# The opening of a sixteen-batch attention kernel: TensorE in text order from its first instruction, and the first batch laid out anew

## The chip, the cores and the metric

The kernel runs on one core of one Trainium2 chip. A core has five engines that run side by side, each through its own instructions in a fixed order, and wait for each other through semaphores: TensorE (PE: matrix products and transposes, weight loads shown apart as PEld), VectorE (DVE), ScalarE (ACT), GpSimd (POOL) and SyncE (SP). Transfers are started by SP, and where rows are picked by an index by GpSimd. The metric is the time of one execution on the device in microseconds (us); less is better. Three runs of the kernel before took 963.57 to 964.73 us, with a median of 963.98.

## The reference

For each of 16 batches with 1024 tokens of width 512, it computes masked self-attention with 8 heads of 64, in which one projection serves as query, key and value, and adds the result to the input:

```python
xt = jnp.transpose(x, (0, 2, 1))
q = xt @ Wq.T
qh = q.reshape(B, T, NH, dk).transpose(0, 2, 1, 3)
scores = scale * jnp.einsum('bhqd,bhkd->bhqk', qh, qh)
cmask = mask[:, None, None, :]
rmask = mask[:, None, :, None]
logits = (scores * cmask + (1.0 - cmask) * NEG) * rmask
attn = jax.nn.softmax(logits, axis=-1)
ctx = jnp.einsum('bhqk,bhkd->bhqd', attn, qh)
ctx = ctx.transpose(0, 2, 1, 3).reshape(B, T, D)
out = ctx @ Wo.T
return jnp.transpose(out, (0, 2, 1))
```

`x` is (16, 512, 1024), the mask (16, 1024) holds zeros and ones, about half of each, and the two weights are 512 x 512. A token whose mask is 0 is no key for anybody; as a query it sees all tokens alike, so its row is the mean.

## The kernel before

**What it does with the mask.** Only tokens with mask 1 ("active") need attention. For each batch the kernel puts the active tokens in front, gathers their rows of `x` from HBM by index (four gathers of 128 rows, and a fifth for a tail where more than 512 are kept), computes attention for 512, 528 or 544 slots and scatters the finished rows back. Rows of masked tokens get the mean instead. Batches run in order of their number of active tokens, so that the widths `wide` can be fixed: the first and the last two are 512 wide.

**The opening** (`run`, up to the loop over batches). The mask arrives; `order` counts the active tokens with eight products of a matrix of ones, forms a key (count times 32 plus the batch's number) and, comparing all keys with all, the rank of each batch. `permute` picks the mask of the batch with a given rank, by a one-hot of the rank; `sources` the number of that batch. `slots_of` turns a mask into slots, by products with a triangular matrix and with ones; `hot` compares each token's slot within its block of 128 with 0 to 127 (one operation on 128 x 1024), and `index` multiplies these one-hots with the token numbers, which gives the list of rows, `idx`. Then come the gathers of batch 0, the transposes `xt` (into two buffers of the pool `ps_0`, then split in a high and a low half of 16 bits, `xh` and `xl`, by `xsplit`), and the query products `query(b, e, g)`: head pair `e`, half `g` of the tokens, 12 products of 16-bit halves each. `qsplit` splits a head pair of q again and spreads it over `xx` by four transfers. `value` transposes q back for the values and sums their squares per head; `peaks`, `top`, `bottom` (together `shift`) take the largest square per head, transpose it, take the largest, and spread it with its sign changed as `nm`: the exponent's bias. `warm` issues products of ones without use, 30 of them, which keep TensorE busy while it has to wait. Meanwhile ScalarE and VectorE split the weights (`wqh`, `wql`), and `sum_half` sums x over the tokens for the mean.

**The loop.** For a batch, `scores(b, p, u)` computes head pair `p` against half of the keys, four tiles that lie over four and a bit of six accumulator banks (`pss`), and four exponentials on ScalarE, each with a running sum; `attend` multiplies these with the values, into banks 4 and 5; `tail_scores` and `attend_tail` do the slots over 512. `recip_sums` and `recip_rows` make one over the sums and bring them to all partitions through HBM (`rr`, `rd`, `rb`), `norm` applies them, `project` multiplies with the output weights and scatters. While batch b runs, the transposes, query products and values of b+1 and the lists of b+2 are put between its scores, by `plan`: 18 steps, each with two places, `(step, half)`. `free` holds what is started at the beginning of a step.

**What sets the order.** A scheduler of the language orders the instructions of an engine by priority and by estimated times; `behind` and `high_priority` steer it, and `once` or `needs` add a wait. From the first score on, TensorE is taken out of it (`manual_schedule`): its instructions stand as the text issues them. In the opening it is the scheduler's. Small products in the loop use a spot in bank 5 (`spot`) or one of two buffers of `ps_m` (`pm`), which they share with the big products.

Waits between `scores` and the exponentials on the same banks: the first product of `scores` waits for the four exponentials before (`self.left`), and the exponentials wait for all products of their `scores`.

## Time and profile before

| | |
|---|---|
| median of three runs | 963.98 us (963.57 to 964.73) |
| profiled execution | 965.21 us, span 963.5 us |
| instructions | 22790 |
| TensorE busy | 931.5 us (97%), 8121 products |
| VectorE busy | 721.1 us (75%) |
| ScalarE busy | 644.7 us (67%) |
| GpSimd busy | 305.1 us (32%) |
| transfers | 176.30 MB, mean 183 GB/s |

The profile is of one execution on the chip. The span runs from the first to the last instruction. A row of the timeline gives the start, the length, the engine, the line of the source and the tile written and read, `tile<-tiles`; in brackets stands how long the engine was idle before and what ended it. A row of waits gives who waited for whom, the sum, how many times, and the longest. A row of stretches gives the busy time of each engine between two moments. Lengths of products overlap, since they are pipelined: twelve that take 0.27 us each start 0.11 us apart.

### The profile page before, as it was taken

What the parts mean: (1) busy time and instruction counts of PE and PEld (TensorE: products, weight loads), DVE (VectorE), ACT (ScalarE), POOL (GpSimd) and SP (SyncE); (2) the same over time, 40 slices, a digit from 0 to 9 for tenths busy, and PEclk for the clock granted to TensorE, in tenths of its full rate; (3) what the DMA queues carried; (4) which work ended last, traced back from release to release, by engine and by line L of the source; (5) the groups of instructions that cost most, each with busy time, mean ns of one, the idle gap of its engine ahead of it and who ended that gap; (6) DMA issues with size and microseconds to landing.
All of it is one profiled execution on the core that took longest, in us unless ns stands there. A gap on an engine that the chain in (4) does not pass through costs nothing.

```text
span 963.5 us, 22790 instructions
## 1 busy us (share of the span) xinstructions
PE 931.5 (97%) x8121; PEld 581.3 (60%) x8121; DVE 721.1 (75%) x2443; ACT 644.7 (67%) x1669; POOL 305.1 (32%) x311
## 2 busy tenths in 40 slices
PE   6799999999999999999999999999999999999997
PEld 4556656566666666666666566666666666565543
DVE  7779677776777767887678687877877788685563
ACT  4778766667677666776767678665767866665651
POOL 2102022142241513415144250522515135252452
PEclk9999999999999999999999999999999999999999
DMA  5756556556675666756656787654767757555552
GB/s 172 222 175 203 155 154 183 163 180 190 180 209 148 194 197 193 220 157 199 177 181 204 198 239 223 177 158 136 214 168 233 243 144 207 151 161 161 171 175 102
DMA packets 78568, 176.30 MB, mean 183 GB/s; under 512 B 14480, under 2 KB 22416, under 8 KB 78448
## 3 DMA queue, kind: packets, MB, share of 16 engines
q1 hardware_dynamic: 57392, 107.09, 39.8%
q0 software_dynamic: 21056, 67.68, 22.4%
q8 instruction: 66, 1.08, 0.5%
q14 instruction: 54, 0.44, 0.2%
HBM read 91.36 MB, written 33.91 MB: 130 GB/s over the span
## 4 chain that ended last, share of the span: by engine, by line
PE 81%; DVE 10%; ACT 4%; DMA 2%; issue 2%; SPq 1%; POOL 0%; POOLq 0%; DVEq 0%; ACTq 0%
PE pss L858 22%; PE pss L823 17%; PE pm L982 17%; PE pm L591 16%; ACT p L838 2%; PE pss L876 2%; PE pm L562 2%; DMA xx<-hl 1%; PE pss L766 1%; PE pm L654 1%; DVE xl L521 1%; PE pss L982 1%; DVE xa L988 1%; PE pm L912 1%; DVE p L777 1%
## 5 line engine op out<-in xcount | busy, mean ns | idle before, releaser
L838 ACT ACTIVATE p<-pss,nm 128x528 f32<-128x528 f32 (+2 forms) x512 | 353.9, 702 | 104.7 <-PE pss L823 101.5
L858 PE MATMUL pss<-p,v 128*64 128x264 f32 (+2 forms) x2048 | 242.4, 389 | 0.0
L823 PE MATMUL pss<-xx 128*128 128x118 f16 (+17 forms) x1856 | 213.6, 287 | 3.9 <-ACT p L838 2.8
L1051 POOL DMA_INDIRECT y_out<-xa,idx x68 | 82.0, 1206 | 405.2 <-DVE nq L732 85.1
L858 PEld LDWEIGHTS pss<-p,v 128*64 128x64 f32 x2048 | 141.4, 137 | 85.8 <-issue 4.9
L823 PEld LDWEIGHTS <-xx 128*128 128x128 f16 (+1 forms) x1856 | 103.2, 96 | 85.1 <-issue 34.3
L591 PE MATMUL pm<-xh,wqh 128*128 128x264 f16 (+5 forms) x512 | 141.8, 277 | 3.3 <-DVE xl L521 1.3
L591 PE MATMUL pm<-xh,wql 128*128 128x264 f16 (+5 forms) x512 | 141.1, 275 | 0.0
L591 PE MATMUL pm<-xl,wqh 128*128 128x264 f16 (+5 forms) x512 | 140.9, 275 | 0.0
L591 PEld LDWEIGHTS <-wqh 128*128 128x128 f16 x1024 | 96.4, 97 | 31.6 <-issue 12.6
L458 POOL DMA_INDIRECT xa<-x_in,idx x68 | 72.5, 1066 | 123.4 <-DMA y_out<-xa,idx 49.1
L838 ACT ACTIVATION_READ_ACCUMULATOR p<-pss,nm 128x1 f32 x512 | 105.2, 205 | 0.0
L982 PE MATMUL pm<-woh,ch 128*128 128x512 f16 x240 | 91.1, 380 | 0.0
L982 PE MATMUL pm<-woh,cl 128*128 128x512 f16 x240 | 90.9, 379 | 0.0
L982 PE MATMUL pm<-wol,ch 128*128 128x512 f16 x240 | 90.9, 379 | 0.0
L595 ACT ACTIVATE q<-pm 128x264 f32<-128x264 f32 (+5 forms) x128 | 50.8, 397 | 43.1 <-PE pm L591 42.7
L988 DVE SCALAR_TENSOR_TENSOR xa<-pm,xa 128x512 f32<-128x512 f32 x61 | 41.6, 681 | 46.0 <-PE pm L982 45.7
L1051 POOL DMA_INDIRECT y_out<-xi,idx x60 | 64.9, 1081 | 33.9 <-PE pss L766 13.4
L658 ACT COPY v<-pm 128x512 f32<-128x512 f32 x64 | 37.5, 586 | 56.0 <-PE pm L654 54.3
L982 PEld LDWEIGHTS <-ch 128*128 128x128 f16 x480 | 44.9, 98 | 47.5 <-issue 4.1
L458 POOL DMA_INDIRECT xi<-x_in,idx x60 | 59.4, 990 | 21.6 <-issue 15.8
L881 ACT COPY c<-pss 128x528 f32<-128x528 f32 (+2 forms) x64 | 38.3, 598 | 37.9 <-PE pss L876 26.8
(249 smaller groups left out, 1485.0 us busy)
## 6 DMA issues: line engine op xcount, KB each, us to landing
xm<-x_nat_in SPq DMA_DIRECT2D x60, 512.0 KB
xx<-hl SPq DMA_DIRECT2D x208, 136.0 KB
rb<-rd SPq DMA_DIRECT2D x72, 132.0 KB
xx<-hl SPq DMA_DIRECT2D x48, 128.0 KB
pt<-c SPq DMA_DIRECT2D x36, 132.0 KB
pt<-p SPq DMA_DIRECT2D x36, 132.0 KB
rb<-rd SPq DMA_DIRECT2D x32, 136.0 KB
ub<-ud SPq DMA_DIRECT2D x16, 256.0 KB
```

The source lines that it names most:

```text
L458: dma = self.nc.gpsimd.indirect_dma_start(out=tile[:n], out_offset=None, in_=self.x, in_offset=bass.IndirectOffsetOnAxis(ap=idx, axis=0))
L562: self.pe = nc.tensor.transpose(pt[:, c, :], x[:n, c * P:(c + 1) * P], self.ident[:n, :n]).ins
L591: self.beat = nc.tensor.matmul(pq, lhsT=w[:, c, e * P:(e + 1) * P], rhs=xx[:, c, cols], start=(k == 0), stop=(k == 3 * DC - 1)).ins
L595: nc.scalar.activation(s["q"][:, e, cols], pq, AF.Copy, scale=1.0 / (SX * SW))
L658: nc.scalar.copy(v, pv)
L823: m = nc.tensor.matmul(flat[:, c0:c1], lhsT=w, rhs=x, start=banks[n] not in banks[:n], stop=banks[n] not in banks[n + 1:])
L838: e = nc.scalar.activation(t, flat[:, at:at + A], AF.Exp, bias=s["nm"][p // 2][:, p % 2 * 2 + k:p % 2 * 2 + k + 1], scale=SCALE, accum_out ...
L858: mm = nc.tensor.matmul(pav[k * DK:(k + 1) * DK, g], lhsT=s["v"][p][:, i, k * DK:(k + 1) * DK], rhs=ps[k, i][:, cols], start=(i == 3), sto ...
L881: self.context_out = nc.scalar.copy(c[:, :A].rearrange("p (g c) -> p g c", g=2), pav).ins
L982: mm = nc.tensor.matmul(po[:cols.stop - cols.start], lhsT=a[:, e, cols], rhs=w[:, e, :], start=(e == 0 and k == 0), stop=(e == DC - 1 and ...
L988: return self.nc.vector.scalar_tensor_tensor(x, po, 1.0 / (SX * SW), x, ALU.mult, ALU.add).ins
L1051: dma = self.nc.gpsimd.indirect_dma_start(out=self.out, out_offset=bass.IndirectOffsetOnAxis(ap=idx, axis=0), in_=x, in_offset=None)
```

## The change

It touches the opening, the first batch, and a few places of all batches.

- TensorE is in text order from its first instruction (`manual_schedule` moves ahead of `order`). The text of the opening is rearranged to be that order, with 22 warm-ups instead of 30.
- Batch 0's mask comes from the least key, not from the ranks: `least` is the smallest key, `is_equal` with it picks the mask. Its number follows as the least key minus 32 times its count, in `slots_of`. The ranks (`ranks`) and `sources` of the others come later.
- In `slots_of` the one-hot comparison of 128 x 1024 becomes eight of 128 x 128 with a scalar per partition, and each of the eight products of `index` waits for its own.
- `slots_of(1)` stands behind the first transposes; the constants of `setup3` (`quad`, `two`, `par`, `low`, `sign`) get a place of their own in the text. The values of head pairs 0 and 1 of batch 0 go to `ps_0`, behind the query products of pair 1. The five gathers of batch 1 come after the query products of pair 2.
- The largest score of batch 0 (`peaks` and `top`, then `bottom`) is issued between its first score products, after the second and the sixth (`between`).
- In batch 0 (`alone`) a score product that begins a bank waits for the exponential of that bank only, exponentials for the products of their own bank only, and they are issued as the banks get done.
- `slots` and `facts_end` use the spot in bank 5 rather than a `pm` buffer, with the reads ahead of other work; `seen` notes these reads.
- The loads of `wo` and of x for the sums, in batch 0, wait for the last product issued (`beat`) rather than for the largest score, and those of `wo` go to steps 3, 6, 9, 12.
- For every batch but the last, `recip_rows` of head pair 1 moves from the head of step 10 to behind the query product in `(10, 0)` (batch 0: `(11, 0)`), as `turn`. Slots move from `(6, 0)` to `(7, 1)`, and in batch 0 a few places are shifted.

```diff
@@ order
+        self.key = key
+        nc.vector.tensor_reduce(self.least, key, AX.X, ALU.min)
+        each = self.sb([P, TB, B], F16, "hl", 2)
+        nc.vector.scalar_tensor_tensor(each, key.unsqueeze(1).broadcast_to([P, TB, B]), self.least,
+                                       mh.rearrange("p b j -> p j b"), ALU.is_equal, ALU.mult)
+        with nc.allow_low_precision(reason="one of the terms is 0 or 1, the others are 0"):
+            nc.vector.tensor_reduce(self.act16[:, 0], each, AX.X, ALU.add)
+
+    def ranks(self):
+        nc, B, key = self.nc, self.B, self.key
         more = self.sb([P, B, B], F16, "c", 4)
...
@@ slots
-        pr = self.pm([P, B, TB])
...
+        spot = self.spot(NC + B)
+        pr, pn = spot[:, :NC].rearrange("p (b j) -> p b j", j=TB), spot[:, NC:]
...
@@ slots_of
+        if b == 0:
+            who = self.base[:, 0:1]
+            nc.vector.scalar_tensor_tensor(who, n, -32.0, self.least, ALU.mult, ALU.add)
+            nc.vector.tensor_copy(self.first_row[:, 0:1], who[0:1, :])
+            nc.vector.tensor_scalar(who, who, float(T), None, ALU.mult)
...
-        nc.vector.tensor_tensor(self.oht[:, b], oh, self.tok.unsqueeze(2).broadcast_to([P, TB, NB]), ALU.mult)
+        for j in range(TB):
+            nc.vector.tensor_scalar(ol[:, j], self.io128, lo[:, j:j + 1], None, ALU.is_equal)
+            if j == 2:
+                nc.vector.tensor_tensor(self.oht[:, b], oh, self.tok.unsqueeze(2).broadcast_to([P, TB, NB]), ALU.mult)
@@ facts_end
-        pe = self.pm([P, B])
-        nc.tensor.matmul(pe, lhsT=self.on16, rhs=self.whole_masks, start=True, stop=True)
+        pe = self.spot(B)
+        self.spotted(nc.tensor.matmul(pe, lhsT=self.on16, rhs=self.whole_masks, start=True, stop=True))
...
@@ value
-        pv = self.pm([P, 4, P])
+        pv = self.pm([P, 4, P]) if b or e > 1 else self.ps_0.tile([P, 2, D], F32, tag="s", name="pss")[:, 0].rearrange("p (k n) -> p k n", k=4)
@@ scores
+            if alone and self.left:
+                own = (1, 2, 3, 0)[banks[n]]
+                if banks[n] not in banks[:n]:
+                    self.needs(m.ins, self.left[own])
+                self.other_banks(m.ins, *(e for k, e in enumerate(self.left) if k != own))
+            elif n == 0 and self.left:
                 self.needs(m.ins, *self.left)
             last = [m.ins]
+            mms.append(m.ins)
+            if n in self.between:
+                self.between.pop(n)()
...
+            if alone:
+                self.other_banks(e, *(m for m, bank in zip(mms, banks) if bank != j))
@@ attend
-                    self.other_banks(mm.ins, *exps[1 - g:])
-                    if g == 0 and i == 3:
+                    self.other_banks(mm.ins, *exps[(1 - g) * (self.reach > 512):])
+                    if g == 0 and i == 3 and self.reach > 512:
                         self.needs(mm.ins, *exps[:1])
@@ run: the opening
+        stack = ExitStack()
+        stack.enter_context(self.tc.manual_schedule(engines={mybir.EngineType.PE}))
         with self.tc.high_priority(offset=HPO):
             self.order()
-            self.permute(0, 1)
-            self.active(0, 1)
-            self.sources(0, 2)
             self.slots_of(0)
-            self.hot(0)
-        self.warm(6)
+        self.warm(7)
         self.index(0)
...
+        self.warm(12)
+        sums0 = [(0, L(self.sum_half, 0, k)) for k in range(2 * DC)]
+        for _, f in sums0[:4]:
+            f()
+        self.xt(0, 0)
+        with self.tc.high_priority(offset=HPO):
+            self.slots_of(1)
+        self.setup3()
+        self.warm(1)
+        self.xt(0, 1)
+        self.warm(2)
+        self.xt(0, 2)
...
-        first = query(0, 0, 0) + xt(0)[3:] + [(0, L(self.facts, 0, 2))] + query(0, 1, 0) + query(0, 0, 1)
-        sums0 = [(0, L(self.sum_half, 0, k)) for k in range(2 * DC)]
-        split1 = query(0, 1, 1)[1:]
-        first += [(0, index1)] + sums0[:4] + value(0, 0) + g1[:1] + query(0, 1, 1)[:1] + g1[1:2]
-        first += value(0, 1) + split1 + sums0[4:] + query(0, 2, 0) + g1[2:3] + query(0, 2, 1)[:1] + g1[3:4]
-        first += [(0, shift0)]
+        first = query(0, 0, 0) + xt(0)[3:] + query(0, 1, 0) + [(0, index1)] + query(0, 0, 1) + [(0, one_sum)]
+        first += query(0, 1, 1) + value(0, 0) + value(0, 1) + sums0[5:] + query(0, 2, 0) + query(0, 2, 1)[:1] + g1
+        first += [(0, L(self.sources, 2, B))]
...
+        self.between = {1: largest, 5: told}
@@ run: the loop
+                turn = [(0.1, L(self.recip_rows, b, 1))]
...
-                                (5, 1): vt(b, 1) + pk(b, 1), (6, 0): post,
-                                (7, 0): third + q(1, 0) + tp(b, 1), (7, 1): q(1, 1) + P_(0) + bt(b, 1), (8, 0): tc(0) + v(0) + end + rng[:2],
-                                (10, 0): tv(0) + tail + q(2, 0), (11, 0): hot + rng[2:] + early,
+                                (5, 1): vt(b, 1) + pk(b, 1),
+                                (7, 0): third + q(1, 0) + tp(b, 1), (7, 1): q(1, 1) + post + P_(0) + bt(b, 1), (8, 0): tc(0) + v(0) + end + rng[:2],
+                                (10, 0): tv(0) + tail + q(2, 0) + turn, (11, 0): hot + rng[2:] + early,
...
-                                (14, 0): tv(0) + rng[2:] + take[:3], (14, 1): v(1) + q(3, 0) + pk(n, 0),
-                                (16, 0): q(3, 1) + tp(n, 0) + take[3:], (16, 1): bt(n, 0),
+                                (14, 0): tv(0) + rng[2:] + take[:3], (14, 1): v(1) + pk(n, 0),
+                                (16, 0): q(3, 0) + tp(n, 0) + q(3, 1) + take[3:], (16, 1): bt(n, 0),
...
-                        free.setdefault(2, []).append(L(self.load, "o", c, None, first_top))
+                        free.setdefault(3 * c + 3, []).append(lambda c=c: self.load("o", c, None, self.beat))
...
-                            free.setdefault(st + 2, []).append(L(self.recip_rows, b, p))
+                            if p != 1 or n == B:
+                                free.setdefault(st + 2, []).append(L(self.recip_rows, b, p))
```

140 lines of the change are left out of this document (74 added, 66 removed).

## The prediction

> **What bounds the kernel now.** I read the page first (its chain), then the stretches by engine, then TensorE's waits after the opening, then the opening instruction by instruction.
>
> ```profile
> PE 81%; DVE 10%; ACT 4%; DMA 2%; issue 2%; SPq 1%; POOL 0%; POOLq 0%; DVEq 0%; ACTq 0%
> ```
> ```profile
> 0.00:30.00 30.00, 22.09 (x180) 14.37 (x180) 23.64 (x96) 14.34 (x32) 9.33 (x37) 1.00 0.56 162
> 30.00:60.00 30.00, 24.65 (x179) 14.74 (x180) 20.98 (x70) 21.91 (x63) 2.59 (x3) 1.00 0.72 206
> 60.00:77.00 17.00, 16.31 (x159) 10.14 (x156) 15.29 (x61) 13.99 (x37) 1.90 (x2) 1.00 0.77 230
> 77.00:100.00 23.00, 21.78 (x209) 14.12 (x209) 22.25 (x73) 19.23 (x51) 3.11 (x3) 1.00 0.61 175
> 100.00:900.00 800.00, 790.05 (x7039) 500.95 (x7036) 605.30 (x2051) 548.17 (x1417) 261.54 (x241) 1.00 0.64 185
> ```
> Columns: stretch, length, then busy time of TensorE, its weight loads, VectorE, ScalarE, GpSimd. TensorE is the bound from 60 us on. Before that it is idle for 7.91 and 5.35 us, and part of its busy time is filler (the warm-up products). So a microsecond that TensorE does not stand still is a microsecond off the end, unless something else becomes late. VectorE, at 22.25 of 23 us between 77 and 100, is the one that could.
>
> **The change part by part.** *Until the first products.* The chain that gives the first list of row numbers (timeline: start, us, engine, line, operation, and in brackets the idle time before and what ended it):
>
> ```profile
> 6.29 0.29 DVE L227 TENSOR_REDUCE act<-hl 128x8 f16<-128x128 f16 x1
> 7.05 2.72 PE L408 MATMUL warm<-on 128*128 128x512 f16 x6
> 8.58 1.22 DVE L360 TENSOR_TENSOR tmp<-io,lo 128x1024 f16<-128x1024 f16 x1
> 10.21 2.29 PE L408 MATMUL warm<-on 128*128 128x512 f16 x5
> 10.39 0.23 DVE L372 TENSOR_SCALAR idx<-pm,base 128x9 int32<-128x9 f32 x1 [0.45 <-PE pm L369]
> 10.62 0.28 DVE L384 TENSOR_SCALAR hr<-row,n 128x128 f32<-128x128 f32 x1
> 10.91 1.30 POOL L458 DMA_INDIRECT xa<-x_in,idx  x1 [7.11 <-DVE hr L384]
> 12.75 2.97 PE L408 MATMUL warm<-on 128*128 128x512 f16 x13
> 15.55 0.60 PE L562 MATMUL pss<-ident,xa 128*128 128x128 f32 x4
> ```
> ```profile
> DMA to landing us min/median/max: 3.5/4.3/5.1
> ```
> The minimum (`least`) replaces the all-pairs comparison, the rank and the one-hot of the rank ahead of the first mask; the quad/two/low/sign constants slip in between. All pairs, rank, place and product end in 1.9 us from the key to the mask (4.6 to 6.58); minimum, product and the constants should need 1.1 to 1.2, so the mask is 0.7 to 0.9 us earlier. Then the one comparison of 1024 (1.22 us) becomes eight of 128, each followed by its own product. By rows eight cost between 8 × 0.08 (spacing of the smallest ones) and 8 × 0.19 us (L384 starts 0.19 us before its successor); I take 0.1 each, as it is f16. It hardly matters: seven warm-ups at 0.43 us (2.29 us for five, overlapping) stand before the index in a fixed order and end around 9.3. So the list comes at 9.7 instead of 10.39, 0.7 us earlier. [...]
>
> First gather: issued 10.24, landed 3.5 us later, at 13.75. Before, the rows had landed at 14.4 but TensorE was in its 13 warm-ups until the transposes of 15.55. Now 12 of them end near 13.3, and the transposes follow the landings: about 13.9, 15.2, 16.7 (gathers are some 1.3 us apart). `slots_of(1)` moves behind the first transpose, and its DVE work between the splits; the splits of blocks 0 and 1 remain the wait.
>
> ```profile
> 19.06 0.27 PE L591 MATMUL pm<-xl,wqh 128*128 128x256 f16 x1
> 23.92 0.27 PE L591 MATMUL pm<-xh,wql 128*128 128x258 f16 x1
> ```
> The query products ran from 19.06; they now start at about 17.3. Behind them the index of batch 1 waits for its eight comparisons, and block 3's split for those (0.5 us risk). The second query half, which ended at 24.2, ends at 22.2 to 22.9: 1.6 us gained.
>
> *Largest score and first scores.*
> ```profile
> 26.49 0.29 DVE L616 COPY hl<-hl 128x512 f16<-128x512 f16 x1
> 26.60 0.72 SPq L625 DMA_DIRECT2D xx<-hl  x1
> 28.73 0.60 SPq L628 DMA_DIRECT2D xx<-hl  x1
> ```
> ```profile
> 28.73 4.39 DMA xx<-hl
> 75.59 2.67 DMA xx<-hl
> ```
> ```profile
> 33.25 1.13 PE L823 MATMUL pss<-xx 128*128 128x512 f16 x4 [1.03 <-DMA xx<-hl]
> 34.42 0.69 ACT L838 ACTIVATE p<-pss,nm 128x512 f32<-128x512 f32 x1 [2.09 <-PE pss L823]
> 38.02 1.57 PE L823 MATMUL pss<-xx 128*128 128x512 f16 x8 [1.78 <-ACT p L838]
> 39.64 0.69 ACT L838 ACTIVATE p<-pss,nm 128x512 f32<-128x512 f32 x1 [1.67 <-PE pss L823]
> 42.08 0.66 PE L651 MATMUL pm<-ident,q 128*128 128x128 f32 x4 [0.62 <-ACT q L595]
> 43.24 1.57 PE L823 MATMUL pss<-xx 128*128 128x512 f16 x8 [0.50 <-ACT p L838]
> 44.92 0.69 ACT L838 ACTIVATE p<-pss,nm 128x512 f32<-128x512 f32 x1 [1.26 <-PE pss L823]
> 51.46 0.33 PE L912 MATMUL pm<-ident,rcol 128*128 128x128 f32 x1 [1.07 <-DVE xl L521]
> 51.63 1.56 PE L823 MATMUL pss<-xx 128*128 128x512 f16 x8
> 53.30 0.69 ACT L838 ACTIVATE p<-pss,nm 128x512 f32<-128x512 f32 x1 [2.45 <-PE pss L823]
> ```
> The two rows between are of the chain in order of time (start, length). The split of the first head pair ended 2.6 us after the query half (26.8 against 24.2), since batch 1's list, tails and flags sat in between; now it is about the same 2.4 us, but the transfer no longer meets batch 1's gathers, which are issued only behind the query product of the third pair. A transfer took 4.39 us there and 2.67 us elsewhere; I take 2.9. The values of pairs 0 and 1 move behind both query halves, into the first pool's banks; their squares and sums, then the largest score, become the new last link, the transpose and broadcast lying between score products 2 and 6. The four sums of halves on ScalarE (0.6 each) now precede the exponentials; one is between the two query copies. From the query half at 22.6: split at 25.0, last of four issues 2.0 later as before (26.78 to 28.73), landed at 29.9, two score products, the broadcast and its read some 1.0. First exponential at 30.9 instead of 34.42, so 3.5 us gained (1.6 from above, 1.9 here).
>
> After it, each exponential waits for its own bank's products, and each product for its bank's exponential, in place of all four. So the ping-pong shown by 1.78 against 1.67 us mostly closes: TensorE loses about 1.2 us before the fourth exponential, 0.6 at the values of pair 3 and 0.7 at a transpose, against 1.78 + 0.62 + 0.50 + 1.07 = 3.97. That gives 1.5 more. Score products (0, 1, second half) at 46.7 instead of 51.63: **4.9 us** for the opening, between 3.5 and 6. What else moves in the opening, and what hides it. The four weight loads of wo (SP) go behind later products, to steps 3, 6, 9 and 12; ScalarE splits them at 9, 10, 16 and 17, so they cost nothing, but SP's queue now holds the third pair's four spreads behind the first of them, which waits for a query product of pair 3: they are issued at about 33.5 and used by the scores of pair 2 some 20 us later. The last four half-sums' loads (SP) wait for the third transposes instead of two warm-ups behind them, so they start about 1.5 us earlier and are through (5 us for 1 MB) when the first spread is issued. The five gathers of batch 1 (GpSimd) wait for the third pair's query product, about 28 instead of 24.91; the first is transposed at about 37, and even 5.1 us to landing leaves 4. The 16 batches' remaining sources (five DVE instructions) and batch 0 and 1's flags stand just ahead of the first split: 0.3 us, which is in the 2.4. The 512 KB sum on VectorE stands before block 3 of batch 1; about 1 us of cover remains, and the wait at 51.46 comes back if it goes.
>
> *Waits of all later batches.*
> ```profile
> PE pm L912 <- DVE rcol L905: 2.3, 3, 1.2
> PE pm L351 <- DVE xa L988: 2.1, 5, 0.4
> PE pm L254 <- DVE tmp L683: 1.6, 4, 0.4
> PE pm L591 <- DVE rr L917: 1.1, 7, 0.2
> PE pss L727 <- DVE m L717: 0.7, 1, 0.7
> PE pm L982 <- DVE rr L917: 0.6, 4, 0.2
> PE pss L714 <- DVE smcol L708: 0.4, 1, 0.4
> ```
> These are sums in us, times, and the longest. `turn` puts the transposed reciprocals of pair 1 behind a query product: it removes L912's 2.1 us (two of the three) and the 1.7 us of waits for `rr` behind it. Slots in the spot bank remove L254's 1.6. Facts in the spot bank no longer wait for `xa`, but for `nm`, which VectorE makes just behind `xa`: nothing gained of the 2.1, perhaps 0.1 lost five times. The largest score of batch 1 gets a query product before each half: 1.1 gained. Sum 6.5 − 0.5 = 6.0 at most; since VectorE, 76% busy from 100 to 900, is what these waited for, I keep two thirds: **4.1 us** (lower end 0, if each wait returns elsewhere). That the second half of a context product no longer waits for exponentials where a batch is 512 wide (the first and the last two batches) is worth no more than the 0.2 us that I find there; nothing is counted.
>
> **Sum.** 4.9 + 4.1 = 9.0 us against the profiled execution's 965.21 us: 956.2. That execution is 1.2 us over the median of 963.98, so on the median's scale 955.0.
>
> **The rivals.** *The half-speed clock comes back.* Eight warm-ups go, and TensorE stands still for each landing. The rows show five warm-ups in 2.29 us and, 5.7 us after the first one, thirteen in 2.97: it starts at half speed. If it fell back, the query products (twelve start 0.11 us apart) would take up to 1.3 us more each for two or three of them: 2.6 us, 957.6. [...]
>
> *VectorE becomes the bound.* From 60 to 100 us it is busy 37.54 of 40. Closing TensorE's gaps there would only move the wait: the opening yields 4, the rest nothing: 960.0. For it: all seven waits above are for VectorE. Against it: 24% idle from 100 on.
>
> *Slower: the turn.* If `turn` came to delay something in each of 14 batches by as much as the longest L912 wait, 1.2 us, that is 16.8 us lost against 9.0 gained (without L912's and rr's part about 6.5): 974. It decides from 0.5 us per batch. Against it: the reciprocals' only reader is six steps later.
>
> *The order does nothing*: TensorE's new text order equals what the waits force anyway, and the transfers end as before: 963 to 965. Against it: the exponentials' waits on other banks are really gone.
>
> **How the numbers follow.** Forecast 0.62 (951 to 958); VectorE 0.20 (957 to 961); clock 0.07 (956 to 960); turn or another new wait, slower, 0.06; nothing, 0.05. A difference of 0.2% (1.9 us) is about what a measurement here can tell from none. Faster takes the first three, 0.89; same 0.05; slower 0.06. Leaving out under 2 in 10, the range is 951 to 961.
>
> **What would show it.** First list at 9.7, first transposes near 13.9, query products from 17.3, first exponential near 30.9, and scores after it without waits over 1.2 us; L254, rr and L912 gone from TensorE's waits after 53 us, the one for facts still there under `nm`. Wrong if the first exponential is later than 33, if TensorE's idle time between 100 and 900 us stays at 9.95, or if warm-ups or query products show half-speed times after 13.

## The result, and the profile after

The changed kernel takes 959.12 us (median of six runs, 957.52 to 961.27) against 963.89 (six runs, 963.39 to 965.29) for the kernel before: a ratio of 0.9945, with a 95% interval of 0.9931 to 0.9958, so 4.8 us or 0.55% faster. The profiled executions are further apart than the medians, 957.52 (span 955.7) against 965.21 (span 963.5): that of the changed kernel is the fastest of its six, that of the kernel before is 1.3 us over its median. In three of the four later sets of runs the kernel before took 15 to 19 us more than here, and the changed kernel 21 to 28 us more; what that means for the gain is told with the experiments, and times are compared inside a set only.

The chain of the changed kernel, and its stretches (columns as in the prediction):

```profile
PE 81%; DVE 9%; DMA 4%; ACT 4%; issue 1%; SPq 1%; POOL 0%; POOLq 0%; DVEq 0%; ACTq 0%
```
```profile
0.00:30.00 30.00, 23.46 (x185) 15.05 (x185) 24.07 (x121) 16.81 (x40) 8.82 (x36) 1.00 0.59 170
30.00:60.00 30.00, 26.03 (x216) 16.68 (x216) 23.77 (x88) 22.89 (x62) 4.07 (x4) 1.00 0.78 216
60.00:77.00 17.00, 14.34 (x124) 8.26 (x122) 14.36 (x47) 13.54 (x36) 2.85 (x3) 1.00 0.82 255
77.00:100.00 23.00, 22.06 (x214) 15.02 (x215) 20.89 (x71) 19.16 (x50) 2.14 (x2) 1.00 0.59 162
100.00:900.00 800.00, 793.04 (x7078) 502.43 (x7075) 607.93 (x2060) 550.29 (x1423) 266.02 (x245) 1.00 0.63 186
```

Idle time of TensorE is the length less its first number. Up to 60 us it falls from 13.26 to 10.51 us, from 100 to 900 from 9.95 to 6.96. Between 60 and 77 it rises from 0.69 to 2.66: there a part of the gain is given back.

The same can be followed by the start of the exponentials, the first ones of a head pair. Lead is before less after:

| batch, pair | before, us | after, us | lead |
|---|---|---|---|
| 0, 0 | 34.42 | 29.87 | 4.55 |
| 0, 1 | 44.92 | 39.31 | 5.61 |
| 0, 3 | 72.22 | 66.81 | 5.41 |
| 1, 0 | 84.99 | 80.82 | 4.17 |
| 1, 1 | 97.97 | 94.97 | 3.00 |
| 3, 0 | 206.38 | 201.60 | 4.78 |
| 7, 0 | 442.31 | 435.54 | 6.77 |
| 13, 0 | 792.30 | 783.94 | 8.36 |
| last one | 941.75 | 934.27 | 7.48 |

So the opening brings 5.4, the stretch from the last head pair of batch 0 to the second of batch 1 takes back 2.4, and the later batches bring 4.5.

*The opening.* Timeline rows of the changed kernel that the prediction named:

```profile
2.62 0.23 DVE L205 TENSOR_SCALAR given<-mt 128x128 f16<-128x128 f32 x1 [1.40 <-DMA mt<-mask_t_in]
4.41 0.29 DVE L217 TENSOR_REDUCE act<-hl 128x8 f16<-128x128 f16 x1
6.70 0.57 DVE L338 TENSOR_SCALAR tmp<-io,c 128x128 f16<-128x128 f16 x3
7.33 0.90 DVE L338 TENSOR_SCALAR tmp<-io,c 128x128 f16<-128x128 f16 x5
8.56 0.23 DVE L397 TENSOR_SCALAR idx<-pm,base 128x9 int32<-128x9 f32 x1 [0.33 <-PE pm L394]
13.16 0.63 PE L595 MATMUL pss<-ident,xa 128*128 128x128 f32 x4 [0.92 <-DMA xa<-x_in,idx]
16.07 0.27 PE L624 MATMUL pm<-xh,wqh 128*128 128x256 f16 x1
27.59 0.59 PE L853 MATMUL pss<-xx 128*128 128x512 f16 x2
28.22 1.30 PE L853 MATMUL pss<-xx 64*128 64x512 f16 x4
29.87 0.69 ACT L877 ACTIVATE p<-pss,nm 128x512 f32<-128x512 f32 x1 [0.99 <-DVE nm L760]
33.56 0.93 PE L853 MATMUL pss<-xx 128*128 128x512 f16 x5 [0.90 <-ACT p L877]
37.43 0.66 PE L684 MATMUL pm<-ident,q 128*128 128x128 f32 x4 [1.01 <-ACT q L628]
42.02 0.66 PE L595 MATMUL pm<-ident,xa 128*128 128x128 f32 x4 [1.51 <-DVE xl L554]
46.74 1.03 PE L853 MATMUL pss<-xx 128*128 128x512 f16 x4
```

The score products at 27.59 have no wait in front: the transfers of `xx` that they read have landed. The first exponential waits for the exponent's bias `nm` instead. Behind it TensorE stands 0.90, 1.01 and 1.51 us where it stood 1.78, 0.62, 0.50 and 1.07.

*The place of the give-back.* The load of 512 KB for a sum over tokens (`xm`) now holds up the two engines that sum it. Rows of the changed kernel's timeline, then its chain in order of time (start, length):

```profile
73.07 1.06 ACT L528 ACTIVATE xm<-xm 128x1024 f32<-128x1024 f32 x1 [2.62 <-DMA xm<-x_nat_in]
75.22 0.69 DVE L674 TENSOR_TENSOR tmp<-v 128x512 f32<-128x512 f32 x1 [2.50 <-ACT v L691]
77.17 0.30 PE L747 MATMUL pss<-ident,smcol 128*128 128x128 f32 x1 [2.64 <-DVE smcol L741]
```
```profile
51.52 5.04 DMA xm<-x_nat_in
71.88 6.66 DMA xm<-x_nat_in
78.56 1.22 DVE ms L535
```

The first three rows are one sequence. ScalarE stands 2.62 us at the sum of a half; behind it in its queue is the copy of `v`; VectorE waits 2.50 for that copy, and TensorE 2.64 for the largest score that VectorE makes from it. From 28 to 100 us, engines stood 4.9 us in four waits for `xm`; before, 1.1 in one. The sum of these waits is not the loss, though: a second profile of the kernel before (`base`, below) shows 3.9 us in three such waits, and its stretch from (0, 3) to (1, 1) takes 25.97 us, as the 25.75 of the first. What seems to count is whether the largest score of batch 1 stands behind the wait.

*The later batches.* TensorE's waits between 100 and 900 us (sum, times, longest), all that are listed:

```profile
PE pss L375 <- DVE nm L760: 2.5, 5, 0.5
PE pm L956 <- ACT q L628: 1.9, 4, 0.5
PE pm L956 <- DVE rcol L949: 1.1, 1, 1.1
PE pm L595 <- DMA xa<-x_in,idx: 0.3, 1, 0.3
PE pm L624 <- DVE xl L554: 0.3, 1, 0.3
```

Two rows of the kernel before in the same stretch, for comparison:

```profile
PE pm L912 <- DVE rcol L905: 2.1, 2, 1.2
PE pm L591 <- DVE xl L521: 1.1, 2, 0.7
```

The waits for `tmp` (1.6) and `rr` (1.1 and 0.6) are gone, those for `rcol` are down from 2.1 to 1.1 and those for `xl` from 1.1 to 0.3, and the facts wait 2.5 for `nm` in place of 2.1 for `xa`. New is a wait of 0.5 us, four times, of the turned reciprocals (L956) for ScalarE's copy of q out of the bank that they share.

### The profile page after: what moved, and what is told of

The parts are those of the page before. It is cut to its first block, busy times and chain, and to the rows that moved or that the text cites. A ratio compares the mean times of both kernels' runs of the same rounds, so it can differ in the third digit from the quotient of the medians.

```text
span 955.7 us, 22822 instructions
## 1 busy us (share of the span) xinstructions
PE 928.0 (97%) x8113; PEld 580.4 (61%) x8113; DVE 719.3 (75%) x2460; ACT 645.4 (68%) x1669; POOL 306.7 (32%) x311
## 3 DMA queue, kind: packets, MB, share of 16 engines
q0 software_dynamic: 21056, 67.68, 22.2%
## 4 chain that ended last, share of the span: by engine, by line
PE 81%; DVE 9%; DMA 4%; ACT 4%; issue 1%; SPq 1%; POOL 0%; POOLq 0%; DVEq 0%; ACTq 0%
PE pss L902 21%; PE pm L1027 17%; PE pss L853 17%; PE pm L624 16%; PE pss L920 2%; ACT p L877 2%; PE pm L595 2%; DVE xl L554 1%; DMA xm<-x_nat_in 1%; PE pm L687 1%; DMA xx<-hl 1%; PE pss L796 1%; DMA xa<-x_in,idx 1%; PE pss L1027 1%; PE pm L956 1%
## 5 line engine op out<-in xcount | busy, mean ns | idle before, releaser
L1096 POOL DMA_INDIRECT y_out<-xa,idx x68 | 79.3, 1166 | 411.1 <-DVE nq L762 114.3
L628 ACT ACTIVATE q<-pm 128x264 f32<-128x264 f32 (+5 forms) x128 | 50.8, 398 | 43.2 <-PE pm L624 43.0
```

The lines of the kernel that those rows point to most:

```text
L628: self.copied = nc.scalar.activation(s["q"][:, e, cols], pq, AF.Copy, scale=1.0 / (SX * SW)).ins
L1096: dma = self.nc.gpsimd.indirect_dma_start(out=self.out, out_offset=bass.IndirectOffsetOnAxis(ap=idx, axis=0), in_=x, in_offset=None)
```

## The experiments

The theory: the gain is that of the opening, less what the 512 KB loads give back, plus what the slots and the turn bring later. The rival for the give-back is VectorE being full; for the later gain, that slots or turn bring nothing by themselves.

### First set: three parts of the change, one at a time

`again` is the changed kernel as it is, for comparison on the same chip.

> The changed kernel once more, unaltered, for a second profile. Theory A (the first mask's landing, not the change, gave 1.0 us of the profiled gain): the landing of the first mask moves between executions by about 1 us (2.62 us in the first profile of the changed kernel, about 3.6 before), and the gain counted from that landing is again 3.5 us at the first exponential, about 4.4 at the last head pair of batch 0, about 2.0 at the second pair of batch 1 and about 6.5 at the end. Rival B (the first profile's gain is all of the change): the mask lands at 2.6 again and the end is 7.5 us earlier again. The median over the rounds is expected 4 to 6 us under the kernel before.

`loads_free` lets batch 0's loads of `xm` wait for the first largest score, as before, and not for the latest product:

```diff
- ... else lambda x=x, c=c: self.load_all(x, c, self.beat))
+ ... else lambda x=x, c=c: self.load_all(x, c, self.st[0]["top"]))
```

> The 512 KB loads of x in batch 0 wait for the first largest score, as before the change, not for the latest product. Theory A (the changed wait delays these loads, and ScalarE and VectorE stand still for them, 4.9 us in four waits, which makes the largest score of batch 1 2.6 us late): these four waits fall to about 1 us, the wait for smcol at batch 1's largest score goes from 2.6 to under 0.6, and the kernel is 1.5 to 2.4 us faster than the changed one (median about 957). Rival B (VectorE is the bound between 60 and 95 us, whatever the loads do): TensorE's wait moves to another VectorE result of the same length, and the time stays within 0.7 us of the changed kernel.

`no_turn` takes out the early turning of pair 1's reciprocals:

```diff
-                 turn = [(0.1, L(self.recip_rows, b, 1))]
+                 turn = []
-                             if p != 1 or n == B:
+                             if True:
```

> The transposed reciprocals of the second head pair stay two steps behind the pair, as before the change. Theory A (the prediction's: the turn removes two of three waits for rcol, 2.1 us, and the 1.7 us for rr, of which two thirds last): 2 to 3 us slower than the changed kernel, rr waits back. Theory B (the trace of after: the turn removes one wait of 1.2 us and the rr waits, and pays four new waits of 0.5 us for the copy of q): 0 to 1.2 us slower. Rival C (the turn costs more than it brings): up to 1 us faster.

`slots_pm` makes the slots of later batches in the two small banks again, at the place of before (the reads behind them lose their priority too):

```diff
-         spot = self.spot(NC + B)
-         pr, pn = spot[:, :NC].rearrange("p (b j) -> p b j", j=TB), spot[:, NC:]
+         pr = self.pm([P, B, TB])
...
-                                 (7, 1): q(1, 1) + post + P_(0) + bt(b, 1),
+                                 (6, 0): post[:len(new[0])],
+                                 (7, 1): q(1, 1) + post[len(new[0]):] + P_(0) + bt(b, 1),
```

> The slots of later batches go back to the two small banks, four steps into the batch, as before the change; all else stays. Theory A (the prediction's: only the 1.6 us of waits for tmp are at stake, two thirds of them): about 1.1 us slower than the changed kernel, in four batches 0.3 to 0.4 each. Theory B (the landmarks of the exponentials: batches 2, 6, 9 and 12, in which slots are made, gain 1.7, 1.8, 1.3 and 0.7 us, so the slots carry nearly all of the later gain): 3.5 to 5 us slower, the loss in just these batches.

Measured, with the kernel before at 978.80 us on this chip:

| | median, us | ratio to before | 95% interval |
|---|---|---|---|
| again | 979.69 | 1.0011 | 0.9987 to 1.0035 |
| loads_free | 975.69 | 0.9971 | 0.9945 to 0.9996 |
| no_turn | 977.54 | 0.9992 | 0.9969 to 1.0016 |
| slots_pm | 980.06 | 1.0014 | 0.9987 to 1.0041 |

The 4.8 us are not there. Of the three parts only `loads_free` is apart from `again` by more than the scatter, 4.0 us faster on the medians. `no_turn` is 2.2 us faster, not slower, and `slots_pm` 0.4 us slower; with runs of one kernel spread over 7 to 11 us neither difference is clear. The waits can be read. First `loads_free` against `again`, TensorE's waits for the largest score of batch 1 (from 60 to 100 us):

```profile
PE pss L747 <- DVE smcol L741: 1.6, 1, 1.6
```
```profile
PE pss L747 <- DVE smcol L741: 2.2, 1, 2.2
```

The upper row is `loads_free`, the lower `again`. Between the exponentials of (0, 3) and (1, 1) `loads_free` takes 26.33 us, `again` 27.92 (the kernel before took 25.75). An earlier start of the loads brings back 1.6 us of this stretch, but does not take the wait away.

Next, TensorE's waits from 100 to 900 us in `no_turn`, and in `slots_pm` (whose line numbers are two lower ahead of its slots):

```profile
PE pm L624 <- DVE rr L961: 1.1, 7, 0.2
...
PE pm L1027 <- DVE rr L961: 0.5, 3, 0.2
```
```profile
PE pm L267 <- DVE tmp L714: 1.6, 4, 0.4
```

Each part moves just the wait that the prediction gave it: without the turn the waits for `rr` are back, with the slots in the small banks the 1.6 us for `tmp`. But in `no_turn` the wait for `rcol` is not back, and the 0.5 us waits of L956 for `q` are gone: the turn does less than its share of the forecast.

### Second set: the kernel before once more, and what is common to the long times

`base` is the kernel before, unaltered, profiled once more; `again2` the changed kernel; `both` joins `loads_free` and `no_turn`.

> The kernel before, unaltered, for a profile on the chip on which the others of this call run. Theory A (the first chip and the second differ in stalls that no semaphore explains, which come on any kernel): its profile shows waits of TensorE put down to issue or to a late ScalarE, of 10 us and more in sum, at other places than in the changed kernel's profile, if this chip is like the second one; on a chip like the first, none, and a span near 963. Rival B (only the changed kernel is open to them): no such waits here, while the changed kernel beside it shows them. Without these waits its time from the first exponential to the last is 907 us either way.

> The changed kernel unaltered, beside the kernel before on the same chip. Theory A (the opening is worth 3.5 to 4.5 us up to the first exponential, 2 to 3 are given back between the last head pair of batch 0 and the second pair of batch 1, the rest brings 3 to 4.5): without stalls the exponentials lead the kernel before's by 3.5 to 4.5 us at the first, 2 to 3 at the second pair of batch 1, 6 to 8 at the end. Rival B (the gains of the first profile are chance): no lead over 2 us at the end.

> The changed kernel with the 512 KB loads of batch 0 behind the first largest score instead of the latest product, and with the transposed reciprocals of the second pair at their old place. Theory A (the two losses seen apart, up to 2.4 us given back at the loads, and 1.9 + 1.0 us of waits before the turned transpose against 1.6 us of rr waits without it, are independent): 2 to 4 us faster than the changed kernel, 5 to 9 faster than before. Rival B (VectorE takes what is freed): within 1 us of the changed kernel.

`alone_off` lets the first products of batch 0 wait for all four exponentials again, not only for those on their own bank:

```diff
-         alone = b == 0
-         if alone and p == 0 and u == 0:
+         alone = False
+         if b == 0 and p == 0 and u == 0:
```

> In batch 0 each exponential waits again for all products of its score step, and the next products for all four exponentials; all else stays as changed. Theory A (the prediction's: waiting by the bank is worth 1.5 us after the first exponential): the time from the first exponential to that of the fourth pair of batch 0 grows from 36.9 by about 1.5 us. Theory B (ScalarE, busy without a gap over 0.8 us from 29.9 to 44.6 us, bounds this stretch, so the waits only change their place): it grows by less than 0.5 us.

With the kernel before at 982.38 us:

| | median, us | ratio to before | 95% interval |
|---|---|---|---|
| base | 983.33 | 1.0004 | 0.9980 to 1.0028 |
| again2 | 986.87 | 1.0041 | 1.0009 to 1.0072 |
| both | 984.25 | 1.0015 | 0.9987 to 1.0043 |
| alone_off | 988.90 | 1.0063 | 1.0035 to 1.0090 |

Here the changed kernel is the slower one by 0.4%. `alone_off` takes 42.37 us from the exponentials of (0, 0) to those of (0, 3), `again2` 41.38: 1.0 us, between what the two theories gave, and 2.0 us on the medians with overlapping intervals. The changed kernel alone takes from 38.86 (`again`) to 41.38 us for the same piece under these conditions, so a difference of 1.0 does not show what the own-bank waits are worth.

The records show what is common to these longer executions. ScalarE stands for up to 4.6 us waiting for something that the profile cannot name ("remote"). ScalarE's waits of that kind over the whole span, in `base`, and in the changed kernel as run in the third set (`again3`):

```profile
ACT c L881 <- remote: 8.3, 2, 4.3
```
```profile
ACT c L925 <- remote: 15.4, 4, 4.6
ACT q L628 <- remote: 4.2, 3, 2.5
ACT p L877 <- remote: 2.5, 1, 2.5
ACT v L691 <- remote: 0.4, 1, 0.4
```

In the first pair of profiles, before and after, there is no such wait. In `base` the first one comes only after batch 1, and up to the last head pair of batch 1 its exponentials start within 0.13 us of those in the first profile. In all ten kernels of these three sets that have the new opening ScalarE stops right behind the third exponential, at 32 to 36 us, and TensorE then stands 2.5 to 4.7 us. In eight of them ScalarE's stop is 1.5 to 3.3 us and "remote"; in `again` and `no_turn` it is 1.0 us, put down to a transpose on TensorE, with 0.4 us of "remote" behind it.

### Third set: what the stop in the opening does, and whether its place is the program's

`again3` is the changed kernel. `shift22` puts 22 copies of one element into ScalarE's stream ahead of the first scores; if the stop belonged to a place in ScalarE's instructions, it would move to an earlier operation of the kernel:

```diff
+        early = self.fixed("early", [P, 24], F16)
+        for k in range(22):
+            self.nc.scalar.activation(early[:, k:k + 1], self.on16[:, :1], AF.Copy)
```

`best` is `shift22` with the edits of `loads_free` and `no_turn`.

> The changed kernel unaltered, as the reference of this call. On a chip like the second and the third, ScalarE stands still for 1 to 3.5 us behind the third exponential with nothing in the profile that it waits for, TensorE then waits 2.5 to 4.3 us, and the granted clock between 35 and 45 us is below 1. On a chip like the first, none of that, and the time is about 959.

> 22 one-element copies are put at the head of ScalarE's instructions, where it waits for the first weights; nothing else changes, so every later instruction of ScalarE stands 22 places further on in its stream. Theory A (ScalarE's unexplained stops sit at fixed places of its instruction stream, some 105 profiled instructions apart, because the next block of instructions comes late when the transfer engines are full): the stop behind the third exponential moves 22 instructions ahead, to the copies of q and v at 21 to 24 us, where the transfer engines are idle, and is gone or under 0.5 us; TensorE's wait before the second score step falls from 2.5 to 4.3 us to about 0.9, the clock stays 1.00 from 35 to 45 us, and the third pair's exponentials come 2 to 3 us earlier than in the reference. Rival B (the stop belongs to the moment, full transfer engines at 32 to 36 us, not to the instruction): it stays at 32 to 36 us, with the clock below 1.

> The 22 copies, the loads behind the first largest score, and the old place of the second pair's transposed reciprocals together. Theory A (the three losses are independent): 4 to 6 us faster than the changed kernel on a chip with the stops, 2 to 3 on one without. Rival B (the stops only move to the next boundary of the stream): within 2 us of the changed kernel.

With the kernel before at 982.97 us: `again3` 984.95, ratio 1.0028 (0.9997 to 1.0059); `shift22` 986.30, 1.0049 (1.0029 to 1.0069); `best` 982.04, 0.9990 (0.9963 to 1.0017).

Timeline rows of `again3`, and then its stretches (the two numbers ahead of the last two are busy GpSimd and the granted clock):

```profile
32.24 0.81 PE L853 MATMUL pss<-xx 128*128 128x512 f16 x3
34.99 0.38 ACT L628 ACTIVATE q<-pm 128x256 f32<-128x256 f32 x1 [2.53 <-remote]
37.06 1.58 PE L853 MATMUL pss<-xx 128*128 128x512 f16 x5 [4.01 <-ACT p L877]
```
```profile
30.00:35.00 5.00, 3.05 (x22) 1.86 (x21) 3.95 (x15) 2.22 (x8) 3.91 (x4) 1.00 0.82 236
35.00:40.00 5.00, 2.94 (x12) 1.27 (x13) 1.95 (x4) 3.39 (x9) 0.00 (x0) 0.60 0.73 202
40.00:45.00 5.00, 5.00 (x30) 3.52 (x28) 3.29 (x12) 3.32 (x10) 0.00 (x0) 0.72 0.53 165
```

The first measurement's profile of the changed kernel has in the same place:

```profile
35.00:40.00 5.00, 3.99 (x31) 2.56 (x29) 3.63 (x13) 4.14 (x13) 0.00 (x0) 1.00 1.04 285
```

The stop costs twice. TensorE stands 4.01 us, and its granted clock is 0.50 from 36.0 to 42.9 us: the five products at 37.06 take 1.58 us where they took 0.93 at 33.56 in the first measurement. All ten profiles with the new opening in these sets show a clock between 0.51 and 0.85 from 35 to 40 us; `base` shows 1.00. By the exponentials of (0, 1) the lead of the changed kernel over the kernel before, 5.61 us in the first measurement, is 3.14, 0.37 and 0.64 us in `again`, `again2` and `again3`. From the exponentials of (0, 0) to those of (0, 1) these three take 2.1 to 4.6 us more than the 9.44 of the first measurement. By the medians the change is worth 5.7, 9.3 and 6.8 us less in these sets than in the first, so the stop in the opening explains a third to two thirds of that. Later stops, which fall elsewhere in each execution, probably make up the rest; that is not worked out.

In `shift22` the stop is 2.38 us in front of the same copy of `q` (L628, now at 36.28), so the place in ScalarE's stream is not its cause. `best` is 2.9 us faster than `again3` on the medians, and `both` was 2.6 faster than `again2`; the forecasts for independent losses were 4 to 6 and 2 to 4 us, and with runs of one kernel spread over more than 10 us neither theory is decided.

### Fourth set: gathers of batch 1 apart

ScalarE's long stops lay in, or behind, rows of gathers; in the changed kernel batch 1's five gathers stand in one row just where the stop is. `apart` spreads them among other work, as they were before, and has the edits of `both`:

```diff
-   first += ... value(0, 1) + sums0[5:] + query(0, 2, 0) + query(0, 2, 1)[:1] + g1
+   first += ... value(0, 1) + g1[:1] + sums0[5:] + query(0, 2, 0) + g1[1:2] + query(0, 2, 1)[:1] + g1[2:3]
-   plan = {(0, 0): query(0, 3, 0) + value(0, 2) + rng0,
+   plan = {(0, 0): g1[3:4] + query(0, 3, 0) + value(0, 2) + g1[4:] + rng0,
```

> The same as the run called both, but the five gathers of batch 1 are no longer issued in one row behind the third pair's query products: the first goes behind the query products of the second pair, the second and third behind those of the third pair, the last two behind the first query product of the fourth pair, so that in the opening no more than two follow one another without a pause. Theory A (TensorE stops, on some chips, at the end of a row of three or more gathers issued without a pause; each stop of 0.8 us and more in the profiles of this study lies in or right behind such a row): no stop behind the third exponential, TensorE's wait before the second score step at most 1.3 us instead of 2.5 to 4.3, clock 1.00 from 35 to 45 us, and the first exponential of the second pair at 39 to 41 us instead of 43.4 to 44.6; later stops, at later rows of gathers, stay. Rival B (the stop belongs to the dense row of query products, or to the transfers of the first pairs): it stays at 32 to 36 us with 2 us and more, and the clock falls again. On a chip without stops the two can't be told apart, and the kernel is 5 to 9 us faster than before.

Measured: 962.14 us against 966.27 for the kernel before, ratio 0.9959 (0.9946 to 0.9972). The profile of `apart` has no such stop, and the kernel before was within 2.4 us of its first median, so this set says nothing of their cause; that stays open. The runs of this set and of the first carry the same chip number, 4, so by that number the stops come and go on one chip and are no mark of it. It gives three other things.

First, most of the gain is there again when the stops are not, even with parts of the change undone.

Second, the price of gathers beside the spreads. The chain of `apart` in order of time, and its first scores:

```profile
26.30 4.10 DMA xx<-hl
32.72 0.78 ACT p L877 x2
```
```profile
30.54 0.59 PE L853 MATMUL pss<-xx 128*128 128x512 f16 x2 [1.66 <-DMA xx<-hl]
```

The transfer takes 4.10 us, as the 4.39 of before, and TensorE waits for it. The first exponential starts 2.85 us later than in the changed kernel. Part of that is a long first operation on VectorE (last section). The three profiles with the new order of gathers and the same long operation (`again2`, `no_turn` and `slots_pm`) have their first exponential at 31.14 to 31.23 us, so that 1.5 us are left for the transfer; the forecast was 1.9.

Third, that the loads' wait has another exit. VectorE in `apart`:

```profile
80.22 1.22 DVE L535 TENSOR_REDUCE ms<-xm 128x1 f32<-128x1024 f32 x1 [3.30 <-DMA xm<-x_nat_in]
81.36 0.28 DVE L750 TENSOR_REDUCE m<-pss 128x1 f32<-128x128 f32 x1
```

This load was issued at 73.66 and landed 6.54 us later. VectorE stands 3.30 us for it with the largest score (L750) behind it in its queue, and TensorE then waits 2.9 us for L750. The stretch from (0, 3) to (1, 1) takes 29.49 us, longer than in the changed kernel (28.16). A part of this is slower score products: behind that wait fourteen of them take 2.86 us (from 82.33), where sixteen take 1.71 us in the changed kernel (from 79.08). So tying the loads to the first largest score, as before, does not by itself remove the give-back (in `both` and `best`, with the same edit, the stretch takes 27.69 and 29.74 us).

SP's order goes with it, however. In the kernel before, both times, and in `loads_free`, the eighth of these loads is issued ahead of four spreads of `xx`, within 0.5 us of the first exponential of (0, 3): at 72.20 with spreads from 75.04 on, 72.08 from 74.7 on, and 72.02 from 73.2 on. These three have the shortest stretches, 25.75 to 26.33 us. In all other eleven profiles it is issued behind these spreads, 4.2 to 5.6 us after that exponential (changed kernel: 71.88, spreads from 68.77 on), and the stretch takes 26.54 to 32.47 us. No run varied this place alone.

## Why the prediction was right, and where its terms were off

The forecast was 955.0 us, in a range of 951 to 961, and faster; the measured 959.12 lies in the range, with about half of the gain (4.8 of 9.0). The terms:

| term | forecast, us | measured, us |
|---|---|---|
| first exponential | 3.5 | 4.55; 3.2 to 3.3 where VectorE's first operation is long, as in the kernel before |
| scores (0, 1, second half) | 4.9 | 4.9 (51.63 to 46.74) |
| batch 1 | 0 | −2.4 |
| later batches | 4.1 | 4.5 |
| sum, profiled executions | 9.0 | 7.5 at the last exponential, 7.8 in the span |

The measured parts add up to 7.0; the other 0.5 is won between the scores of (0, 1) and the exponentials of (0, 3). In the forecast, two thirds of 6.0 are 4.0 rather than 4.1.

*Until the first products.* The list came at 8.56, forecast 9.7. The mask ends 1.9 us earlier (4.70 against 6.58). Of this, 1.0 is the first operation on VectorE, which starts 0.2 us earlier and takes 0.23 us in this execution against 1.06 in that of before; the 0.85 that is left for the key's minimum is what was forecast (0.7 to 0.9). The eight comparisons take 1.4 us for what I put at 0.8, and start 0.16 to 0.17 us apart: near the upper end of 0.19 from the row of L384. That f16 would bring each to 0.1 was my estimate, which no row had shown; each is 0.25 us long. The eight cost more than the one operation of 1.22. The fixed order of the warm-ups cost nothing beyond that: the seven started 1.9 us earlier too and end at 8.32, and the last comparison ends at 8.23.

*Largest score and first scores.* The order of the late links was wrong. The query products started 1.2 us earlier than forecast, yet the second half ended at 23.4 and not at 22.2 to 22.9. The transfer, forecast to land at 29.9, was off the chain by 27.59; the four half sums on ScalarE, named as preceding the exponentials, and `nm` behind them are what the first exponential waits for. That moving batch 1's gathers away frees the transfer is shown by `apart`. The ping-pong mostly did not close: TensorE stands 3.4 us at the places where it stood 3.97, so 0.6 came of the 1.5. Its larger remaining wait is for `xl` (1.51), which is not a wait between banks. That the 4.9 for the opening came out exactly is luck: an earlier start made up for that.

*The step that failed* is that of the 512 KB sums. The prediction said "about 1 us of cover remains, and the wait at 51.46 comes back if it goes" and costed it at nothing. The cover went, not at 51.46 but 25 us later. The price is 2.4 us. That VectorE or ScalarE stands behind the loads, and TensorE's largest score behind them, is shown by the rows. Why the loads come late is only in part: the new wait for the latest product was the suspect, but with the old wait the give-back was smaller in `loads_free` and as large in `both`, `best` and `apart`. The place of the eighth load behind the spreads in SP's order, which the prediction did not look at, fits all fourteen profiles, if narrowly (26.33 against 26.54 us), and was not tested alone.

*Waits of all later batches.* The sum came out (4.5 for 4.1), by luck, since its parts were not right. In batches 2, 6, 9 and 12, where slots are made, the changed kernel gains 1.7, 1.8, 1.3 and 0.7 us: together 5.4, and the other batches from 3 to 13 lose 0.7. In `apart`, which has the slots but not the turn, batch 2 to 13 take 703.35 us, against 706.20 before and 701.43 after. The slots and what goes with them are therefore worth 2.9 us, not 1.1 to 1.6: besides the 1.6 for `tmp`, most of the 1.1 for `xl` and the 1.2 us wait for `rcol` in batch 2 are gone without the turn. By this pair the turn nets 1.9, not 2.5. Of that, 1.4 is one wait of `apart` for the largest score in batch 12; with its own waits of 0.5 us behind ScalarE's copy, it loses 0.4 us in each of batches 5, 8, 11 and 13. These are single profiles of different sets, and parts under 0.5 us are not told apart by them; on the medians of the first set the kernel without the turn was even 2.2 us faster, which is not clear of the scatter. Two of the signs that the prediction named did not come: a wait of 1.51 us is left after the first exponential, and the transposed reciprocals (L912, now L956) are not gone from TensorE's waits but stand at 3.0 us (1.9 and 1.1) against 2.1. The facts' wait moved to `nm` and grew from 2.1 to 2.5, the loss that was forecast.

*The rivals.* VectorE as the bound gave 960.0, near the measured median, but by another way: from 60 to 77 us VectorE is busy 14.36 of 17, less than before, and what stops TensorE is a queue standing behind a load. The slower turn and the order that does nothing are excluded by the rows. The clock rival was no part of the first measurement (clock 1.00 from 10.7 us, where its record begins, to 952.7), and came true in the later sets, with a trigger that the prediction had not: its 2.6 us were worked out for query products, while the stop and the clock together took 2.1 to 4.6 us between the exponentials of (0, 0) and (0, 1).

*Open:* what the stops are, and why the new opening has one at its third exponential in all ten of these profiles, while the one profile of the old opening has none. "Faster by 0.55%" is what the first measurement shows; in the three sets with stops the change gains nothing (1.0011, 1.0041 and 1.0028, of which only 1.0041 excludes 1). No version is shown to beat the changed kernel in a quiet run: `apart` was not run beside it, and the interval of its ratio overlaps that of the change. In the sets with stops every version with the loads behind the first largest score was faster than the changed kernel of its set: `loads_free` by 4.0 us, `both` by 2.6, `best` by 2.9. Only the first is clear of the scatter, and the other two also lack the turn.

## What to carry to other kernels

When a change speeds up one stage, look at the loads whose start is tied to that stage's work, or whose issue stands behind other transfers in one queue, and whose consumers stand early in an in-order queue: time won in the stage is lost where the queue stands for them (2.4 us here), and the engine that shows the wait (TensorE here) is two steps away from the load. Move work out of a shared small bank before reordering it: by the profiles the slots' own bank brought more here than the turned reciprocals (2.9 us against 1.9). And an opening with less slack should be measured on more than one occasion, beside the kernel before each time, since it can be faster in a quiet run and lose all of it when a stop of a few microseconds falls into it (TensorE stood 2.5 to 4.7 us here).

## What the runs showed of the hardware

*The first operation on VectorE takes 0.23 us or 1.1.* In `again2` it starts 0.17 us later than in the changed kernel's first profile (2.62, above), and is five times as long:

```profile
2.79 1.11 DVE L205 TENSOR_SCALAR given<-mt 128x128 f16<-128x128 f32 x1 [1.56 <-DMA mt<-mask_t_in]
```

In all 14 profiles it takes 0.23 to 0.27 us when it starts by 2.74 us (eight of them) and 1.06 to 1.12 us when it starts from 2.77 on (six). The long ones end near 3.9 us; GpSimd's small fills, one behind the other, begin their last one at 3.71. No run takes the fills away, so it is not shown that they lengthen the operation. Later VectorE operations of the changed kernel's first profile (`quad` at 2.77, 0.28 us, and `two` at 3.52, 0.21 us) run beside the same fills without such a length; in `again2` `quad`, at 2.93, takes 0.97 us. In the changed kernel the 1.0 us passes on to the first exponential (30.25 to 30.44 us with a short one in `again`, `again3`, `loads_free` and `both`; 31.14 to 31.23 with a long one in `again2`, `no_turn` and `slots_pm`; with 22 copies in ScalarE's stream 30.93 in `best` with a short one, 31.69 in `shift22` with a long one), in the kernel before not (34.30 with a short one in `base`, 34.42 with a long one). That may be why the changed kernel's six runs spread over 3.7 us and those of before over 1.9; it was only argued.

*The clock falls behind some stops of TensorE and not behind others.* TensorE stood 4.01 us in `again3` (33.05 to 37.06), and the granted clock was 0.50 from 36.0 to 42.9. It also stood only 2.5 us in `again`, and the mean clock was 0.68 from 35 to 40 us. A stop of 2.64 us in the changed kernel's first profile (74.54 to 77.17) left it at 1.00 (stretches 60 to 77 and 77 to 100 us, in the section on the result). The means of the ten profiles with the stop at the third exponential, and the time at the lower clock estimated from them, with the 0.50 of `again3` as the lower value in all:

| | clock, 35 to 40 us | clock, 40 to 45 us | at 0.50, us (estimate) |
|---|---|---|---|
| again | 0.68 | 0.97 | 3.5 |
| loads_free | 0.81 | 0.85 | 3.4 |
| no_turn | 0.76 | 0.90 | 3.4 |
| slots_pm | 0.70 | 0.96 | 3.4 |
| again2 | 0.85 | 0.81 | 3.4 |
| both | 0.51 | 0.80 | 6.9 |
| alone_off | 0.75 | 0.91 | 3.4 |
| again3 | 0.60 | 0.72 | 6.8 |
| shift22 | 0.85 | 0.80 | 3.5 |
| best | 0.74 | 0.92 | 3.4 |

TensorE stood 4.0 us in `loads_free` as in `again3`, and the clock was down half as long. So the length of the stop alone does not tell these profiles apart; what does was not shown.
